# Cross-attention on one core: column maxima straight from PSUM in the first batch, and two block sums put behind the evictions

## Chip, cores and metric

The kernel runs on one core of a Trainium2 chip. The metric is the device time of one execution in microseconds (us). The engines are PE (matmuls), DVE (element-wise work on vectors), ACT (copies, exponentials, bias), POOL (reductions over partitions) and SP, which here only issues DMAs. Each engine runs its own queue in order.

## What is computed

The reference, cut to what matters; B = 8, C1 = C2 = 512, N = 1024, D = 64, all in fp32:

```python
q = einsum('bcn,dc->bnd', x1, Wq) + bq
k = einsum('bcn,dc->bdn', x2, Wk) + bk[:, None]
v = einsum('bcn,dc->bdn', x2, Wv) + bv[:, None]
attn = softmax(einsum('bnd,bdm->bnm', q, k), axis=2)
return einsum('bcm,bnm->bcn', v, attn) + x1
```

The kernel keeps the scores transposed: m lies on the partitions, in eight tiles of 128, and n on the columns, in two halves of 512. The softmax over m therefore needs a maximum and a sum over tiles and over partitions. It also multiplies in another order: y = x2 times the exponentials, scaled by the reciprocals of the sums, and then o = Wv y + bv + x1.

## The kernel before

Each batch is a `Batch` object `s` with its tiles. `head` (L349) does the first work of batch 0; then `period` (L431) runs once per batch and works on batch `s`, while it prepares the next one, `n`. The schedule is manual: the order in which the program issues instructions is the order of each engine's queue, and waits between engines follow from the tiles.

*Scores.* `scores(s, h, i)` (L164) makes the two score tiles of a pair: half h of the columns, pair i of 0 to 3, and groups g = 0, 1 of the rows, which come from the two row halves of PE at once (64 rows each). The pair goes either into one tile of the pool `ps_s`, which has two slots of two PSUM banks each (tag "sc"), or into two banks of the pool `ps_a`, "a0" and "a1" or "c0" and "c1". It returns `copy`, with which ACT moves the pair to SBUF, into `e[h]`; a pair in one tile takes one copy of 1024 columns (L189), a pair in two banks takes two of 512 (L187). All eight PSUM banks are used this way.

*Maximum and exponential.* `fold` (L194) takes the maximum (or the sum) of pairs 0 and i, two groups side by side, 1024 columns at once, on DVE (L201). `fold_halves` (L203) brings the two groups together (L205). `highest` (L207) does so and lets POOL reduce the result over the partitions (L210). Then the maximum is subtracted on DVE and ACT takes the exponential: `first_exponentials` for half 0 of batch 0 (L221, 512 columns each, L224 and L225), `exponentials` elsewhere (L227).

*Products.* The products y and o are made by a scheme of seven block products in place of eight (`MULT`, L259). Left blocks are quarters of x2 (`a`) or of Wv (`w`), with sums S1 to S4 (`left_sums`, L91; on DVE, L100); S3 is written over block 21, and S4 reads S2. Right blocks are quarters of the exponentials (`t`) or of y, with sums T1 to T4 (L233). `multiply` (L269) runs one block product into bank pair a or c of `ps_a`; `first(i)` and `second(i)` in `period` are the products for y and for o. The first product of y, `first(1)`, opens bank pair a, `first(2)` opens c. `evict_o(s, "12")` (L319) reads bank pair a and `evict_o(s, "21")` reads c, each with two instructions at L324; half 21 has two more additions at L331. Each eviction then issues its two stores on SP.

*The head.* `head` loads x1 of batch 0 into `x1_head` and x2 into `x2_head`, which holds the buffer of tag "e1". `head_queries` (L339) makes q of one half of the columns: eight matmuls, each in two passes on PE, in two column groups at once, then one ACT instruction that adds the bias (L347). Its bank is "c1" for half 0 and "a0" for half 1. The order in `head` from L384 is: q of half 0, the keys, the four pairs of scores of half 0 (pairs 0 and 1 in `ps_s`, pair 2 in a, pair 3 in c), the copy of pair 0, the first maximum with pair 1 read from PSUM, the copies of pairs 2, 3 and 1, two more maxima, `highest`, the sums S1 and S2, q of half 1, the load of x for the next batch, three pairs of scores of half 1, the eight exponentials of half 0, and last the copies of half 1. `first(1)` of `period` follows on PE and reads the first four exponentials.

*The end of a period.* In the first period the four sums S1 to S4 of the next batch stand at L529, after `evict_o(s, "22")` and ahead of the last two evictions. In later periods these sums are made earlier (L491 and L503).

Of the kernel before, what the change touches and what calls it, by code (L numbers as in the profile page):

```python
# [9 lines left out]
F32 = mybir.dt.float32  # L10
AF = mybir.ActivationFunctionType
ALU = mybir.AluOpType
# [3 lines left out]
def kernel(  # L16
# [40 lines left out]
    nc = tc.nc  # L57
    P = 128
    B, C, N = x1.shape
# [64 lines left out]
    def sum_a(s, *ks):  # L124
        for k in ks:
            if k != "S3":
                s.a[k] = sb.tile([P, MH, C // 2], F32, tag=f"a{k}", name=f"a{k}_{s.b}")
        left_sums(s.a, *ks)
# [35 lines left out]
    def scores(s, h, i, bank=None):  # L164


        if i == 0:
            s.e[h] = sb.tile([P, 2, MH, H], F32, tag=f"e{h}", name=f"e_{s.b}_{h}")
        e = s.e[h]
        if bank:  # L170
            whole = None
            ps = [
                ps_a.tile([P, H], F32, tag=f"{bank}{g}", name=f"ps_s{bank}{g}_{s.b}_{h}_{i}")
                for g in range(2)
            ]
        else:
            whole = ps_s.tile([P, 2, H], F32, tag="sc", name=f"ps_s_{s.b}_{h}_{i}")
            ps = [whole[:, g, :] for g in range(2)]
        for g, r in ((0, lo), (1, hi)):
            nc.tensor.matmul(  # L180
                ps[g], s.k[r, ts(i, P)], s.q[r, ts(h, H)], start=True, stop=True
            )

        def copy():
            if bank:
                for g in range(2):
                    nc.scalar.copy(e[:, g, i, :], ps[g])  # L187
            else:
                nc.scalar.copy(e[:, :, i, :], whole)  # L189

        copy.ps = whole
        return copy

    def fold(s, h, i, kind, op, ps=None):  # L194

        e = s.e[h]
        if i == 1:
            s.mx[h] = sb.tile([P, 2, H], F32, tag="fold", name=f"{kind}_{s.b}_{h}", bufs=2)
        f = s.mx[h]
        new = e[:, :, i, :] if ps is None else ps  # L200
        nc.vector.tensor_tensor(f, e[:, :, 0, :] if i == 1 else f, new, op)  # L201

    def fold_halves(s, h, op):  # L203
        f = s.mx[h]
        nc.vector.tensor_tensor(f[:, 0, :], f[:, 0, :], f[:, 1, :], op)  # L205

    def highest(s, h):  # L207
        fold_halves(s, h, ALU.max)
        s.top[h] = sb.tile([P, H], F32, tag="top", name=f"top_{s.b}_{h}", bufs=2)
        nc.gpsimd.partition_all_reduce(s.top[h], s.mx[h][:, 0, :], P, ReduceOp.max)  # L210

# [124 lines left out]
            fold(s, h, i, "sum", ALU.add)  # L336
        total(s, h)

    def head_queries(s, x_sb, h, bank):  # L339

        ps = ps_a.tile([P, H], F32, tag=bank, name=f"ps_q_{s.b}_{h}")
        for c in range(CT):
            for r in (lo, hi):
                nc.tensor.matmul(
                    ps[r, :], wq_sb[:, c, :], x_sb[:, c, ts(h, H)], start=(c == 0), stop=(c == CT - 1)
                )
        nc.scalar.activation(s.q[:, ts(h, H)], ps, AF.Identity, bias=bq_sb)  # L347

    def head(s):  # L349

        s.q = sb.tile([P, N], F32, tag="q", name=f"q_{s.b}", bufs=2)
        x1_sb = sb.tile([P, CT, N], F32, tag="x", name="x1_head")
        x2_sb = sb.tile([P, 2, MH, H], F32, tag="e1", name="x2_head")
        s.x = x2_sb.rearrange("p a (b t) n -> p (a b) (t n)", t=2)

        def load_x1(c, h):  # L360
            nc.sync.dma_start(
                x1_sb[:, c : c + 2, ts(h, H)],
                x1[s.b, c * P : (c + 2) * P, ts(h, H)].rearrange("(t p) n -> p t n", p=P),
            )

        nc.gpsimd.dma_start(bqk_sb, bqk)
        nc.gpsimd.dma_start(bv_sb, bv)
        nc.scalar.dma_start(wqk_sb, wqk)
        warm = const.tile([P, P], F32, name="warm")
        nc.vector.memset(warm, 0.0)  # L370
        ps = ps_a.tile([P, H], F32, tag="a0", name="ps_warm")
        for _ in range(WARM):
            nc.tensor.matmul(ps[:, 0:P], warm, warm, start=True, stop=True)
        load_x1(0, 0)
        load_x1(2, 0)
        for c in range(CT):
            nc.sync.dma_start(s.x[:, c, :], x2[s.b, ts(c, P), :])
        nc.scalar.activation(warm[:, 0:1], warm[:, 0:1], AF.Exp)
        load_a(s, "11")
        load_x1(0, 1)  # L380
        load_x1(2, 1)
        load_a(s, "21", "22", "12")
        load_values()
        head_queries(s, x1_sb, 0, "c1")  # L384
        keys(s, "c0")
        copies = [scores(s, 0, i, bank) for i, bank in enumerate((None, None, "a", "c"))]
        copies[0]()
        fold(s, 0, 1, "max", ALU.max, copies[1].ps)
        for i in (2, 3, 1):
            copies[i]()  # L390
        fold(s, 0, 2, "max", ALU.max)
        fold(s, 0, 3, "max", ALU.max)
        highest(s, 0)
        sum_a(s, "S1", "S2")
        head_queries(s, x1_sb, 1, "a0")
        load_x(states[1], x1)
        copies = [scores(s, 1, 0), scores(s, 1, 1), scores(s, 1, 2, "c")]
        for g in range(2):
            for i in range(MH):
                first_exponentials(s, g, i)  # L400
        for copy in copies:
            copy()
        fold(s, 0, 1, "sum", ALU.add)
        fold(s, 0, 2, "sum", ALU.add)
        fold(s, 1, 1, "max", ALU.max)
        fold(s, 0, 3, "sum", ALU.add)
# [24 lines left out]
    def period(s, n, nn, nnn):  # L431

        def first(i):
            multiply(s, "y", i, s.a, s.t, MH)

        def second(i):
            multiply(s, "o", i, w, s.y, 2)

        open_t(s)
        first(1)
        if s.b == 0:
            head_second(s, n)
        sum_e(s, "T1", "T2")
        if s.b == 0:
            total(s, 0)
        else:
            sum_e(s, "T4")
        if n:  # L450
            load_a(n, "11")
        first(2)
        if s.b == 0:
            keys(n)
            load_x(nn, x1)
            evict_y(s, "11", (1,))
            sum_e(s, "T4")
            shares(s, 0)
            evict_y(s, "11", (2,))
        else:  # L460
            shares(s, 0)
            evict_y(s, "11")
        sums(s, 1)
        sum_e(s, "T3")
        shares(s, 1)
        if n:
            load_a(n, "12", "21", "22")
        first(6)

        def next_queries():  # L470
            queries(nn)
            load_x(nn, x2)

        def next_keys():
            keys(nn)
            if nnn:
                load_x(nnn, x1)

        if n:
            scores_and(n, 0, "c", next_queries if nn else nothing)  # L480
            for i in range(1, MH):
                fold(n, 0, i, "max", ALU.max)
            highest(n, 0)
        first(5)
        fetch_o(s, "11")
        fetch_o(s, "22")
        if n:
            for i in range(MH):
                exponentials(n, 0, i)
            if s.b:  # L490
                sum_a(n, "S1", "S2", "S3")  # L491
        first(7)
        evict_y(s, "22")
        first(3)
        evict_y(s, "12")
        if n:
            scores_and(n, 1, "a", next_keys if nn else nothing)
            sums(n, 0)
        sum_y(s, "T1")
        sum_y(s, "T2")  # L500
        if n:
            if s.b:
                sum_a(n, "S4")  # L503
            else:
                left_sums(w, "S1", "S2", "S3", "S4")
            for i in range(1, MH):
                fold(n, 1, i, "max", ALU.max)
            highest(n, 1)
        first(4)
        evict_y(s, "21")  # L510
        second(1)
        sum_y(s, "T3")
        sum_y(s, "T4")
        second(6)
        fetch_o(s, "12")
        if n:
            exponentials(n, 1, 0)
            exponentials(n, 1, 1)
        second(2)
        evict_o(s, "11")  # L520
        fetch_o(s, "21")
        second(5)
        if n:
            exponentials(n, 1, 2)
            exponentials(n, 1, 3)
        second(7)
        evict_o(s, "22")
        if s.b == 0:
            sum_a(n, "S1", "S2", "S3", "S4")  # L529
        if n:  # L530
            second(3)
            evict_o(s, "12")
            second(4)
            evict_o(s, "21")
        else:
            second(4)
            evict_o(s, "21")
            second(3)
            evict_o(s, "12")
# [37 lines left out]
```

## Time and profile before

| | us |
|---|---|
| median of three runs | 717.13 (717.10 to 717.17) |
| the profiled execution | 716.93 |
| its span | 714.90 |
| granted clock of PE | 1.00 |
| DMA | 87.39 MB, mean 122 GB/s |

The span is the time from the first to the last instruction of the profiled execution; 2.03 us lie around it. A line of the timeline has start and duration in us, engine, line of the program, operation, written and read tiles, shape, number of instructions, and in brackets the idle time of the engine ahead of it with what ended it. What happens in the head, by the timelines of the engines: the last key matmul starts its group at 12.49, when its load has landed; the keys' bias on ACT ends at 14.31 and the scores of half 0 start at 14.36; q of half 1 runs from 17.99 and its bias from 21.70; POOL's reduction of the maximum takes 2.68 us from 21.72; the first exponential starts at 25.43 and the first product of y at 26.12.

### The profile page before, as it was taken

What the parts mean: (1) busy time and instruction counts of PE and PEld (TensorE: products, weight loads), DVE (VectorE), ACT (ScalarE), POOL (GpSimd) and SP (SyncE); (2) the same over time, 40 slices, a digit from 0 to 9 for tenths busy, and PEclk for the clock granted to TensorE, in tenths of its full rate; (3) what the DMA queues carried; (4) which work ended last, traced back from release to release, by engine and by line L of the source; (5) the groups of instructions that cost most, each with busy time, mean ns of one, the idle gap of its engine ahead of it and who ended that gap; (6) DMA issues with size and microseconds to landing.
All of it is one profiled execution on the core that took longest, in us unless ns stands there. A gap on an engine that the chain in (4) does not pass through costs nothing.

```text
span 714.9 us, 5407 instructions
## 1 busy us (share of the span) xinstructions
PE 705.6 (99%) x1892; PEld 299.8 (42%) x1892; DVE 590.2 (83%) x569; ACT 201.3 (28%) x271; POOL 97.2 (14%) x38
## 2 busy tenths in 40 slices
PE   8999999999999999999999999999999999999997
PEld 4333444434444434444344444443434444444443
DVE  0999899988979888798887987889887898989454
ACT  2733412043211522224231232403324034220010
POOL 0132030030200211021200202002020020301000
PEclk9999999999999999999999999999999999999999
DMA  8577132441333503435133252232601350042004
GB/s 333 210 235 256 68 147 101 156 154 46 147 146 119 189 8 141 148 118 191 58 119 127 109 191 98 108 118 89 220 0 61 117 177 0 0 161 75 0 1 147
DMA packets 34699, 87.39 MB, mean 122 GB/s; under 512 B 3952, under 2 KB 3952, under 8 KB 34672
## 3 DMA queue, kind: packets, MB, share of 16 engines
q1 hardware_dynamic: 33344, 84.95, 33.6%
q10 hardware_dynamic: 1264, 2.10, 0.9%
q8 instruction: 15, 0.25, 0.1%
q14 instruction: 12, 0.10, 0.0%
q0 software_dynamic: 64, 0.00, 0.0%
HBM read 68.42 MB, written 16.78 MB: 119 GB/s over the span
## 4 chain that ended last, share of the span: by engine, by line
PE 87%; DVE 8%; DMA 1%; issue 1%; ACT 1%; SPq 0%; POOL 0%; DVEq 0%; ACTq 0%; POOLq 0%
PE ps_ya L279 27%; PE ps_yc L279 21%; PE ps_oa L279 15%; PE ps_oc L279 11%; PE ps_s L180 5%; PE ps_k L138 3%; PE ps_q L138 3%; DVE max L201 1%; DMA x_head<-in_x_dram 1%; DVE eT L236 1%; DVE e L230 1%; DVE aS L100 1%; PE ps_sa L180 1%; DVE den L219 1%; PE ps_sc L180 1%
## 5 line engine op out<-in xcount | busy, mean ns | idle before, releaser
L215 POOL PARTITION_ALL_REDUCE den<-sum x16 | 65.3, 4081 | 433.2 <-DVE sum L205 433.2
L279 PE MATMUL ps_ya<-eT,aS 128*128 128x512 f32 x256 | 113.1, 595 | 0.0
L279 PE MATMUL ps_yc<-e,a 128*128 128x512 f32 x256 | 112.6, 592 | 0.0
L289 ACT COPY uy<-ps_ya 128x512 f32<-128x512 f32 x48 | 28.1, 588 | 233.2 <-PE ps_ya L279 233.2
L230 DVE TENSOR_TENSOR e<-e,top 128x1024 f32<-128x1024 f32 x60 | 70.0, 1219 | 13.9 <-POOL top L210 13.9
L279 PEld LDWEIGHTS ps_ya<-eT,aS 128*128 128x128 f32 x256 | 48.0, 190 | 63.8 <-issue 63.6
L279 PEld LDWEIGHTS ps_yc<-e,a 128*128 128x128 f32 x256 | 48.6, 190 | 61.6 <-issue 60.1
L324 DVE SCALAR_TENSOR_TENSOR o<-ps_oc,bv_sb,o 128x512 f32<-128x512 f32 x48 | 35.7, 749 | 41.6 <-PE ps_oc L279 41.5
L231 ACT ACTIVATE e<-e 128x1024 f32<-128x1024 f32 x60 | 62.2, 1056 | 22.2 <-DVE e L230 20.4
L289 ACT COPY uo<-ps_oa 128x512 f32<-128x512 f32 x48 | 28.1, 586 | 132.4 <-PE ps_oa L279 131.1
L189 ACT COPY e<-ps_s 128x1024 f32<-128x1024 f32 x47 | 46.7, 1027 | 61.5 <-PE ps_s L180 61.5
L279 PE MATMUL ps_ya<-e,a 128*128 128x512 f32 x128 | 56.4, 594 | 1.3 <-ACT e L225 0.8
L279 PE MATMUL ps_oc<-y,w 128*128 128x512 f32 x128 | 57.5, 592 | 0.0
L279 PE MATMUL ps_oa<-yT,w_S 128*128 128x512 f32 x128 | 57.5, 592 | 0.0
L279 PE MATMUL ps_yc<-eT,a 128*128 128x512 f32 x128 | 57.0, 598 | 0.0
L279 PE MATMUL ps_ya<-e,aS 128*128 128x512 f32 x128 | 56.2, 592 | 0.0
L219 DVE RECIPROCAL den<-den 128x512 f32<-128x512 f32 x16 | 53.6, 3349 | 0.0
L180 PE MATMUL ps_s<-q,k 64*128 64x512 f32 x188 | 47.9, 608 | 1.6 <-ACT q L347 0.8
L210 POOL PARTITION_ALL_REDUCE top<-max x16 | 30.3, 1897 | 131.3 <-DVE max L205 131.3
L308 DVE TENSOR_TENSOR y<-ps_yc,uy 128x512 f32<-128x512 f32 x48 | 31.2, 676 | 15.0 <-PE ps_yc L279 14.9
L201 DVE TENSOR_TENSOR max<-max,e 128x1024 f32<-128x1024 f32 x32 | 39.2, 1225 | 3.7 <-ACT e L187 0.5
L201 DVE TENSOR_TENSOR sum<-sum,e 128x1024 f32<-128x1024 f32 x32 | 39.2, 1225 | 2.1
(65 smaller groups left out, 757.5 us busy)
## 6 DMA issues: line engine op xcount, KB each, us to landing
x_in_x_dram<-in_x_dram SPq DMA_DIRECT2D x56, 512.0 KB, 5.4
a<-in_x2T_dram SPq DMA_DIRECT2D x32, 512.0 KB, 4.2
o<-in_x_dram SPq DMA_DIRECT2D x64, 256.0 KB, 6.4
out_dram<-o SPq DMA_DIRECT2D x64, 256.0 KB, 2.1
x_head<-in_x_dram SPq DMA_DIRECT2D x8, 512.0 KB, 8.0
q<-q ACTq DMA_DIRECT2D x14, 128.0 KB, 6.9
w<-in_wvT_dram SPq DMA_DIRECT2D x4, 256.0 KB, 8.9
wqk_sb<-in_wqk_dram ACTq DMA_DIRECT2D x1, 256.0 KB, 4.7
```

The source lines that it names most:

```text
L138: nc.tensor.matmul(ps[r, :], w_sb[:, c, :], s.x[:, c, ts(h, H)], start=(c == 0), stop=(c == CT - 1),)
L180: nc.tensor.matmul(ps[g], s.k[r, ts(i, P)], s.q[r, ts(h, H)], start=True, stop=True)
L189: nc.scalar.copy(e[:, :, i, :], whole)
L201: nc.vector.tensor_tensor(f, e[:, :, 0, :] if i == 1 else f, new, op)
L215: nc.gpsimd.partition_all_reduce(s.den[h], s.mx[h][:, 0, :], P, ReduceOp.add)
L219: nc.vector.reciprocal(s.rden[h], s.den[h])
L230: nc.vector.tensor_tensor(e, e, top, ALU.subtract)
L231: nc.scalar.activation(e, e, AF.Exp)
L279: nc.tensor.matmul(ps, left[ka][:, k, ts(j, P)], right[kb][:, k, :], start=opens and k == 0, stop=i in (2, 3, 4) and k == n_k - 1, skip_gr ...
L289: nc.scalar.copy(s.tmp[i, j], ps)
L308: nc.vector.tensor_tensor(y[:, j, :], ps, s.tmp[add, j], ALU.add)
L324: nc.vector.scalar_tensor_tensor(o, s.bank[bank, j], bv_sb[:, c : c + 1], o, ALU.add, ALU.add)
```

## The change

In the first batch, the maximum of half 0 is no longer taken pair by pair over 1024 columns. A new `head_max` takes it bank by bank over 512 columns: the first group of pair 0 is copied to SBUF and then the other seven banks are read from PSUM one after the other, always into the same tile. `fold_halves` is left out for this half, since both groups are then in one tile of 512 columns. The second group of pair 0 is copied by ACT after that, then pair 1; pairs 2 and 3 are handed over to the next step.

That step is the new `head_second_scores`. q of half 1 is made in two quarters of 256 columns, each in its own slot of `ps_s` instead of bank "a0". After the bias of each quarter stands the copy of one of the pairs 2 and 3 in ACT's queue. The scores of pairs 0 and 1 of half 1 are then made for the first 256 columns, and after that for the second 256; pair 2 is made as before. The sums S1 and S2 stand after these in the program instead of ahead of them, on DVE with nothing new between.

In the first period, S3 and S4 of the next batch move behind the last two evictions; S1 and S2 stay. This next batch is the second of the eight.

```diff
-        copy.ps = whole
+        copy.ps = ps
         return copy
 
-    def fold(s, h, i, kind, op, ps=None):
+    def fold(s, h, i, kind, op):
...
-        new = e[:, :, i, :] if ps is None else ps
-        nc.vector.tensor_tensor(f, e[:, :, 0, :] if i == 1 else f, new, op)
+        nc.vector.tensor_tensor(f, e[:, :, 0, :] if i == 1 else f, e[:, :, i, :], op)
...
+    def head_max(s, ps):
+
+        s.mx[0] = sb.tile([P, 2, H], F32, tag="fold", name=f"max_{s.b}_0", bufs=2)
+        f = s.mx[0][:, 0, :]
+        for i, new in enumerate(ps[1:]):
+            nc.vector.tensor_tensor(f, f if i else s.e[0][:, 0, 0, :], new, ALU.max)
+
     def highest(s, h):
-        fold_halves(s, h, ALU.max)
+        if s.b or h:
+            fold_halves(s, h, ALU.max)
...
-    def head_queries(s, x_sb, h, bank):
-
-        ps = ps_a.tile([P, H], F32, tag=bank, name=f"ps_q_{s.b}_{h}")
+    def head_queries(s, x_sb, n, ps):
+
         for c in range(CT):
             for r in (lo, hi):
                 nc.tensor.matmul(
-                    ps[r, :], wq_sb[:, c, :], x_sb[:, c, ts(h, H)], start=(c == 0), stop=(c == CT - 1)
+                    ps[r, :], wq_sb[:, c, :], x_sb[:, c, n], start=(c == 0), stop=(c == CT - 1)
                 )
-        nc.scalar.activation(s.q[:, ts(h, H)], ps, AF.Identity, bias=bq_sb)
+        nc.scalar.activation(s.q[:, n], ps, AF.Identity, bias=bq_sb)
+
+    def head_second_scores(s, x_sb, others):
+
+
+
+        halves = slice(H, H + H // 2), slice(H + H // 2, N)
+        for k, n in enumerate(halves):
+            ps = ps_s.tile([P, 2, H], F32, tag="sc", name=f"ps_q_{s.b}_{n.start}")
+            head_queries(s, x_sb, n, ps[:, 0, 0 : H // 2])
+            others[k]()
+        s.e[1] = sb.tile([P, 2, MH, H], F32, tag="e1", name=f"e_{s.b}_1")
+        ps = [ps_s.tile([P, 2, H], F32, tag="sc", name=f"ps_s_{s.b}_1_{i}") for i in range(2)]
+        for k, n in enumerate(halves):
+            for i in range(2):
+                for g, r in ((0, lo), (1, hi)):
+                    nc.tensor.matmul(
+                        ps[i][:, g, ts(k, H // 2)],
+                        s.k[r, ts(i, P)],
+                        s.q[r, n],
+                        start=True,
+                        stop=True,
+                    )
+        last = scores(s, 1, 2, "c")
+
+        def copy():
+            for i in range(2):
+                nc.scalar.copy(s.e[1][:, :, i, :], ps[i])
+            last()
+
+        return copy
...
-        head_queries(s, x1_sb, 0, "c1")
+        head_queries(s, x1_sb, slice(0, H), ps_a.tile([P, H], F32, tag="c1", name="ps_q_head"))
         keys(s, "c0")
         copies = [scores(s, 0, i, bank) for i, bank in enumerate((None, None, "a", "c"))]
-        copies[0]()
-        fold(s, 0, 1, "max", ALU.max, copies[1].ps)
-        for i in (2, 3, 1):
-            copies[i]()
-        fold(s, 0, 2, "max", ALU.max)
-        fold(s, 0, 3, "max", ALU.max)
+        e, ps = s.e[0], copies[0].ps
+        nc.scalar.copy(e[:, 0, 0, :], ps[0])
+        head_max(s, sum((c.ps for c in copies), []))
+        nc.scalar.copy(e[:, 1, 0, :], ps[1])
+        copies[1]()
+        copy = head_second_scores(s, x1_sb, copies[2:])
         highest(s, 0)
         sum_a(s, "S1", "S2")
-        head_queries(s, x1_sb, 1, "a0")
         load_x(states[1], x1)
-        copies = [scores(s, 1, 0), scores(s, 1, 1), scores(s, 1, 2, "c")]
         for g in range(2):
             for i in range(MH):
                 first_exponentials(s, g, i)
-        for copy in copies:
-            copy()
+        copy()
...
         if s.b == 0:
-            sum_a(n, "S1", "S2", "S3", "S4")
+            sum_a(n, "S1", "S2")
         if n:
             second(3)
             evict_o(s, "12")
             second(4)
             evict_o(s, "21")
+            if s.b == 0:
+                sum_a(n, "S3", "S4")
```

## The prediction

> **What bounds the kernel now.** I read the busy times first, then the list of waits of PE, then the chain of waits in the first batch, and last the timeline of DVE and PE at the end of the first period.
>
> ```profile
> span 714.9 us, 5407 instructions
> ...
> PE 705.6 (99%) x1892; PEld 299.8 (42%) x1892; DVE 590.2 (83%) x569; ACT 201.3 (28%) x271; POOL 97.2 (14%) x38
> ```
>
> PE is busy for 99% of the span, so a gain can only be a gap of PE that closes. The list of waits (total, times, longest, in us) names the gaps:
>
> ```profile
> PE ps_ya L279 <- ACT e L225: 0.8, 1, 0.8
> PE ps_s L180 <- ACT q L347: 0.8, 1, 0.8
> ...
> PE ps_ya L279 <- DVE o L324: 0.5, 1, 0.5
> ...
> PE ps_sa L180 <- DVE y L306: 0.2, 1, 0.2
> ```
>
> After 130 us PE waits for nothing. So whatever PE gains before 130 us reaches the end, unless DVE work made late there becomes a new wait. The first two waits lie in the first batch. The chain of waits there (start, us, what):
>
> ```profile
> 18.34 1.24 DVE max L201
> ...
> 19.67 1.24 DVE max L201
> ...
> 21.54 1.23 DVE aS L100
> ...
> 22.79 1.94 DVE aS L100
> 24.74 0.61 DVE e L224
> ...
> 25.43 1.77 ACT e L225 x3
> ```
>
> The reader is to see two things. From the maxima the path runs over DVE (S1, S2, the first subtraction) and ACT's first exponential to PE's first y product at 26.12. And two maxima of which the second reads what the first wrote start 1.33 us apart, though each takes 1.226: the wait of DVE for its own result, next to a wait for another engine (here ACT), costs 0.105. The third wait sits at the end of the first period; DVE and PE in the timeline:
>
> ```profile
> 120.65 1.22 DVE L100 TENSOR_TENSOR a<-a,a 128x1024 f32<-128x1024 f32 x1
> 121.78 1.22 DVE L100 TENSOR_TENSOR aS<-a,aS 128x1024 f32<-128x1024 f32 x1
> 122.92 1.40 DVE L324 SCALAR_TENSOR_TENSOR o<-ps_oa,bv_sb,o 128x512 f32<-128x512 f32 x2
> ```
> ```profile
> 119.61 3.60 PE L279 MATMUL ps_oc<-yT,w 128*128 128x512 f32 x8
> 123.72 7.13 PE L279 MATMUL ps_ya<-e,a 128*128 128x512 f32 x16 [0.51 <-DVE o L324]
> ```
>
> The two lines of L100 are S3 and S4 of the next batch (S1 and S2 ran from 118.25): they stand ahead of the evictions that free PE's bank.
>
> [...]
>
> **Part A, maxima of half 0.** Removed on DVE: three maxima of 1024 columns (16.58 to 20.90, with a hole of 0.54 for an ACT copy) and the fold of halves at 20.93 (0.69). Added: seven maxima of 512 columns, each reading the result of the one before. The first needs half of the first copy: 15.54 + 0.586 (L187, the same shape) + 0.03 = 16.16, against 16.58. The banks are ready before their turn: PE finishes the last score at about 18.1. So the chain's pace decides. A maximum takes 0.68 to 0.69 and waits for DVE's own result and for a PE result that no earlier wait covers: 0.685 + 0.105 = 0.79. The seventh starts at 16.16 + 6 x 0.79 = 20.90 and ends at 21.58; the old fold ended at 21.62. S1 follows 0.60 after the seventh's start, at 21.50 (before 21.54), and POOL's reduction after its end. Gain about 0.05.
>
> The pace is no row of this trace, so bounds: if only DVE's own wait is paid, it is 0.71 (the w sums, 95.25 to 95.96), and S1 starts at 21.02, a gain of 0.5. If nothing is waited for it is 0.60 (L306, two independent ones), and the gain is 1.17. Below, 0.80 with a duration of 0.692 loses 0.02. I take 0.79, because each reading instruction is an in-place update like L201's, where the price was paid.
>
> The order behind it is unchanged: S1, S2 (stretched to 1.94 beside POOL's 2.68), subtraction 3.12 after S1's start, exponential 0.77 later, PE 0.68 after that. All move by the same 0.05.
>
> **Part A, q of half 1 and the scores in halves of columns.** It must only be done before PE is wanted at 26.07. Passes of 512 columns come every 0.43, the last of 128 columns in the warm-up 0.13 apart; 256 columns I put at 0.215, half of 0.43. PE starts q at 17.99 as before (its slot is free at 17.5: the first maximum ends 16.84, ACT's second copy follows). The first half's eight pairs end at about 19.8, the second's last pass starts at 21.32. On ACT, in queue order: the whole copy of pair 1 waits for maximum 3 (18.4) and ends 19.5; bias of q's first half 20.0 to 20.5 (0.689 less 256 columns, 0.21); two copies of pair 2 to 21.5; second half 21.75 to 22.2; two copies of pair 3 to 23.2. Behind them stand the exponentials, due at 25.4: cover 2.2. On PE scores (1,0) start at 21.63, (1,1) after q's second half at 22.27, and (1,2), whose banks ACT frees at 23.2, has its last pass at 24.09. PE is ready at 24.6, 1.45 before the exponential. So the wait for q (0.8) goes, but what is late next is the exponential: worth nothing. No DMA is added; the next batch's x load waits on the same reads of x1_head, whose end stays at 21.7. Inputs are no limit: S1 ran without a DMA wait at 21.54.
>
> **Part B, S3 and S4 of the next batch last.** The two sums at 120.65 and 121.78 (2.27) go behind both evictions. Eviction 12 then starts at 120.65, its banks having been complete since 119.8, and both are free at 122.06, before PE's last pass of second(4) (starting 122.62). The y product starts at 123.05 instead of 123.72, without the first weight load exposed (passes 0.53 apart at that start, 0.43 otherwise): gain 0.67 + 0.10 = 0.77.
>
> What comes late: eviction 21 waits for second(4) to 123.26; two additions of o to 125.2; S3 125.1, S4 126.25, and T1 at 127.4 instead of 126.75, while PE is 0.77 early. T2 is due at first(6), 136.8, and is done at about 132.9: cover 3.9. The rest of DVE runs 0.65 late until it waits for PE anyway, 0.48 at 169.20 and 2.74 at 172.64; there 1.42 is absorbed. S3 is needed at 158, S4 at 165. SP's queue gets its two output stores for half 12 earlier. Without that cover the price would be at most 1.42.
>
> **Sum.** 0.05 + 0.77 = 0.82. The profiled execution took 716.93 (span 714.90 and 2.03 around it), becoming 716.1; the median, 0.20 higher, 717.13 - 0.82 = 716.3.
>
> **Rivals.** No change within what can be told is 0.2%, 1.43 us, so 715.70 to 718.56.
>
> 1. The forecast, 716.3: 0.48.
> 2. The maxima run at 0.71, one wait each: 717.13 - 0.5 - 0.77 = 715.85. For it: the PE results are long there, so that wait may overlap. Against: at L201 the queue paid for both. 0.19.
> 3. They run at 0.60: 717.13 - 1.17 - 0.77 = 715.2; PE would still be ready (24.6) before the exponential (24.9). Against: in-place sums in the trace never come closer than 0.71 at 512. 0.18.
> 4. The period's gain is given back, because DVE, late by 1.42 relative to PE, makes PE wait further on: 717.1. For it: DVE was the late one at 85.95 and 123.72. Against: the cover counted above. 0.07.
> 5. Slower: narrow passes cost more than half. There are 24 pair passes of 256 columns (16 of q, 8 of scores). Extra of 0.06 each uses up PE's 1.45; from 0.095 each the whole change loses; if a pass costs as much as one of 512 columns, 24 x 0.215 - 1.45 = 3.7 is lost, 717.13 + 3.7 - 0.77 = 720.1. For it: weights must load within 0.215, and loads take 0.137 to 0.187. Against: passes 0.13 apart in the warm-up with loads of 128 columns. 0.08.
>
> **Numbers.** Faster by over 0.2%: rival 3 and what of 1 and 2 lies under 715.70, 0.35. Slower: 0.08. Same: 0.57. For eight in ten, from rival 3's edge to rival 4's: 715.0 to 717.0. The forecast's own range is 716.0 to 716.5.
>
> **What would show it.** The seven maxima in the timeline of DVE: 0.79 apart, the last starting near 20.9. The first y product near 26.07, with its wait for the exponential grown from 0.8 to about 1.4, and no wait of scores for q longer than 0.3. At the end of the first period no wait for an eviction. The T sums start 4.4 us after the y product instead of 3.0, and no new PE wait up to 175. Wrong: maxima closer than 0.75, q passes further than 0.25 apart, or a new PE wait after 124.

## The result and the profile after

The changed kernel took 716.26 us (median of 20 runs) against 717.15 for the kernel before (20 runs): a ratio of 0.9986, 95% interval 0.9980 to 0.9992. That is 0.89 us faster, where the forecast was 716.3 and a gain of 0.82. The gain is 0.12%, under the 0.2% that the prediction took as its bound for no change, though with so many runs the interval leaves out 1. The rest of this document is about where the 0.89 lies, and whether it lies where the steps of the prediction put it.

The page of the changed kernel (its span, then busy time, share and instructions of each engine):

```profile
span 714.4 us, 5460 instructions
...
PE 705.5 (99%) x1916; PEld 301.4 (42%) x1916; DVE 590.6 (83%) x572; ACT 201.8 (28%) x273; POOL 97.2 (14%) x38
```

PE's busy time is as before (705.5 and 705.6), with 24 matmuls more: the passes of 256 columns. The span is only 0.5 shorter. But the first scores start at 14.68 here and at 14.36 in the profile before, because the loads of the head landed later in this execution (the last key matmuls, which wait for one, start at 12.81 instead of 12.49). That start varied from 14.36 to 14.83 over the profiles of this study, whatever the kernel, and no part of the change can reach it: all of its work comes after. So I compare places by their distance from the start of the first score matmul (L180), not by the clock of the span.

The list of waits of PE (total, times, longest, in us):

```profile
PE ps_ya L286 <- ACT e L232: 1.3, 1, 1.3
...
PE ps_s L180 <- ACT k L162: 0.8, 1, 0.8
...
PE ps_k L138 <- DMA x_head<-in_x_dram: 0.2, 1, 0.2
```

Of the four waits shown of before, the one for q (0.8) and the one for the eviction (0.5) are gone, and the one for the first exponential grew from 0.8 to 1.3. The one for y (ps_sa, 0.2) is no longer listed, though it is not gone: y12_early, below, takes it up. The wait for the exponential is the first batch's only large wait that the change could touch, and it took over what the wait for q gave up. The chain of waits in the first batch (start, us, what) shows what stands behind it:

```profile
16.47 0.70 DVE max L211
...
17.20 0.02 DVEq L211
...
17.27 0.70 DVE max L211
...
17.99 0.70 DVE max L211
...
18.72 0.02 DVEq L211
...
18.78 0.70 DVE max L211
```

The reader is to see the price of a wait. From one maximum to the next it is 0.80, 0.72 and 0.79. Between the first two and the last two stands a piece "DVEq" of 0.02: in five of the six steps the queue of DVE has an instruction of its own, 21 ns long, for a second wait. By the semaphores in the trace, that piece waits for DVE's own result and the maximum behind it waits for PE. Between the second and the third there is none (that maximum waits for DVE's own result alone), and the step is about 0.07 shorter. The seventh maximum starts at 21.16, which is 6.48 after the first scores; the prediction had 6.54.

At the end of the first period, DVE and PE in the timeline (start, length, engine, line, operation, tiles, count, and in brackets the idle time ahead and its releaser):

```profile
120.87 1.40 DVE L331 SCALAR_TENSOR_TENSOR o<-ps_oa,bv_sb,o 128x512 f32<-128x512 f32 x2
122.19 0.74 DVE L331 SCALAR_TENSOR_TENSOR o<-ps_oc,bv_sb,o 128x512 f32<-128x512 f32 x1
123.47 0.75 DVE L331 SCALAR_TENSOR_TENSOR o<-ps_oc,bv_sb,o 128x512 f32<-128x512 f32 x1 [0.54 <-PE ps_oc L286]
...
125.34 1.22 DVE L100 TENSOR_TENSOR a<-a,a 128x1024 f32<-128x1024 f32 x1
126.48 1.22 DVE L100 TENSOR_TENSOR aS<-a,aS 128x1024 f32<-128x1024 f32 x1
127.61 1.22 DVE L243 TENSOR_TENSOR eT<-e,e 128x1024 f32<-128x1024 f32 x1
```

```profile
119.84 3.60 PE L286 MATMUL ps_oc<-yT,w 128*128 128x512 f32 x8
123.27 7.03 PE L286 MATMUL ps_ya<-e,a 128*128 128x512 f32 x16
```

The evictions of ps_oa now start 2.4 us before PE's y product, and that product starts with no idle time ahead of it. Its group is 7.03 long where it was 7.13: the first weight load starts at 122.84, 0.43 ahead of the first pass, and the second pass comes 0.43 after the first; before, load and pass started together (123.71 and 123.72) and the second pass came 0.53 after the first. S3 and S4 end at 127.70, and the T sums start 4.34 us after the y product (3.03 before; 4.4 was predicted). DVE is late there, and has made up for it some 45 us further on:

```profile
169.29 0.68 DVE L313 TENSOR_TENSOR y<-ps_ya,den 128x512 f32<-128x512 f32 x1
172.09 0.69 DVE L313 TENSOR_TENSOR y<-ps_ya,den 128x512 f32<-128x512 f32 x1 [2.12 <-PE ps_ya L286]
```

Where DVE waited 0.48 and 2.74 us for PE before, it waits 0 and 2.12: the lateness went into idle time of DVE, and PE waits for nothing after 124 us.

### The profile page after: what moved, and what is told of

It is laid out like the page before. It is cut to its first block, busy times and chain, and to the rows that moved or that the text cites. A ratio compares the mean times of both kernels' runs of the same rounds, so it can differ in the third digit from the quotient of the medians.

```text
span 714.4 us, 5460 instructions
## 1 busy us (share of the span) xinstructions
PE 705.5 (99%) x1916; PEld 301.4 (42%) x1916; DVE 590.6 (83%) x572; ACT 201.8 (28%) x273; POOL 97.2 (14%) x38
## 4 chain that ended last, share of the span: by engine, by line
PE 88%; DVE 8%; DMA 1%; ACT 1%; issue 1%; SPq 0%; POOL 0%; DVEq 0%; ACTq 0%; POOLq 0%
PE ps_ya L286 27%; PE ps_yc L286 21%; PE ps_oa L286 15%; PE ps_oc L286 12%; PE ps_s L180 5%; PE ps_k L138 3%; PE ps_q L138 3%; DMA x_head<-in_x_dram 1%; DVE eT L243 1%; DVE e L237 1%; DVE max L200 1%; PE ps_sa L180 1%; DVE den L226 1%; DVE aS L100 1%; PE ps_sc L180 1%
## 5 line engine op out<-in xcount | busy, mean ns | idle before, releaser
L189 ACT COPY e<-ps_s 128x1024 f32<-128x1024 f32 x44 | 43.7, 1027 | 60.0 <-PE ps_s L180 59.1
L180 PE MATMUL ps_s<-q,k 64*128 64x512 f32 x180 | 45.9, 607 | 0.8 <-ACT k L162 0.8
L243 DVE TENSOR_TENSOR eT<-e,eT 128x1024 f32<-128x1024 f32 x32 | 38.9, 1255 | 0.5
```

Source lines behind the costliest of these rows:

```text
L180: nc.tensor.matmul(ps[g], s.k[r, ts(i, P)], s.q[r, ts(h, H)], start=True, stop=True)
L243: nc.vector.tensor_tensor(t[k], t[x], t[y], ALU.subtract)
```

## The experiments

All times are medians, each beside that of the kernel before, timed together with it. The ratio is taken over the runs themselves and can differ a little from the quotient of the medians. Distances are from the first score matmul in the profiled execution: to the first y product, to the keys that PE makes in the middle of the first period (the group of L138 near 88 us), to the first y product of the second period, and to the start of the last matmul.

| kernel | us | before | ratio, 95% interval | first y | keys | second y | last matmul |
|---|---|---|---|---|---|---|---|
| before | | 717.15 | | 11.76 | 74.10 | 109.36 | 695.55 |
| after | 716.26 | 717.15 | 0.9986 [0.9980, 0.9992] | 11.60 | 74.00 | 108.59 | 694.68 |
| a_only | 717.05 | 717.12 | 1.0004 [0.9996, 1.0012] | 11.60 | 73.99 | 109.24 | 695.43 |
| b_only | 716.46 | 717.12 | 0.9992 [0.9984, 1.0001] | 11.75 | 74.07 | 108.66 | 694.75 |
| unsplit | 716.24 | 717.12 | 0.9987 [0.9980, 0.9993] | 11.59 | 73.97 | 108.56 | 694.65 |
| two_chains | 715.65 | 717.12 | 0.9982 [0.9975, 0.9988] | 10.95 | 73.33 | 107.92 | 694.01 |
| y12_early | 715.42 | 717.20 | 0.9974 [0.9964, 0.9983] | 11.60 | 72.92 | 107.51 | 693.60 |
| both | 714.70 | 717.20 | 0.9965 [0.9952, 0.9977] | 10.94 | 72.21 | 106.80 | 692.89 |
| all_last | 716.39 | 717.20 | 0.9991 [0.9982, 0.9999] | 11.59 | 73.98 | 108.57 | 694.66 |
| both_unsplit | 714.79 | 717.23 | 0.9967 [0.9954, 0.9979] | 10.95 | 72.41 | 107.00 | 693.09 |
| s2_late | 715.01 | 717.23 | 0.9972 [0.9961, 0.9982] | 10.73 | 72.79 | 107.38 | 693.47 |

### One part at a time: a_only and b_only

a_only is the changed kernel with the order of S1 to S4 put back:

```diff
-            sum_a(n, "S1", "S2")
+            sum_a(n, "S1", "S2", "S3", "S4")
...
-            if s.b == 0:
-                sum_a(n, "S3", "S4")
```

> The changed kernel with part B undone: the new head, S3 and S4 ahead of the evictions again. My theory: 0.05 to 0.2 us faster than before, 716.95 to 717.1, with the wait for the eviction (0.5) back. Rival, that the head gives the gain: about 716.3.

b_only is the kernel before with the same two places changed the other way.

> The kernel before with part B alone: S3 and S4 of the next batch go behind the last two evictions, the head stays as it was. My theory, that most of the gain is the wait for eviction 12 at the end of the first period: 0.7 to 0.8 us faster than before, about 716.4, no PE wait for an eviction at 123, the wait of scores for q (0.8) still there. Rival, that the gain is the head's closed wait for q: no faster than 717.0.

The ratios alone don't settle how the gain is divided: both intervals reach 1, and a gain of 0.1 can't be told from none in the medians. The distances and the waits do. The list of waits of a_only:

```profile
PE ps_ya L286 <- ACT e L232: 1.3, 1, 1.3
...
PE ps_ya L286 <- DVE o L331: 0.5, 1, 0.5
```

and of b_only:

```profile
PE ps_ya L279 <- ACT e L225: 0.8, 1, 0.8
...
PE ps_s L180 <- ACT q L347: 0.8, 1, 0.8
...
PE ps_sa L180 <- DVE y L306: 0.3, 1, 0.3
```

With part A alone the wait for the eviction stands as before, and the last matmul comes 0.12 earlier. With part B alone the head's waits stand, and the last matmul comes 0.80 earlier. Together 0.92; the changed kernel has 0.87. So the parts add, and B is nine tenths of the change.

### Are the narrow pieces worth anything: unsplit

The changed kernel with q of half 1 and its scores made over 512 columns again, in one slot of ps_s, between the copies of pairs 2 and 3:

```diff
-        for k, n in enumerate(halves):
-            ps = ps_s.tile([P, 2, H], F32, tag="sc", name=f"ps_q_{s.b}_{n.start}")
-            head_queries(s, x_sb, n, ps[:, 0, 0 : H // 2])
-            others[k]()
...
+        others[0]()
+        ps = ps_s.tile([P, 2, H], F32, tag="sc", name=f"ps_q_{s.b}_1")
+        head_queries(s, x_sb, slice(H, N), ps[:, 0, :])
+        others[1]()
+        copies = [scores(s, 1, 0), scores(s, 1, 1), scores(s, 1, 2, "c")]
```

> The changed kernel with q of half 1 and its scores in whole columns (512) again; q takes a slot of the score pool, its bias stands between ACT's copies of pairs 2 and 3. My theory, that PE has 1.4 us to spare ahead of the first exponential: the same time as the changed kernel (within 0.1 us), the wait for q back at about 0.8 and the wait for the exponential down from 1.3 to about 0.7. Rival, that the narrow pieces carry the head's gain: 0.8 us slower than the changed kernel, the wait for the exponential as it was.

It takes 716.24, the same as the change within what can be told, and its first y product is at 11.59 instead of 11.60. Its waits of PE:

```profile
PE ps_s L180 <- ACT q L353: 0.8, 1, 0.8
PE ps_ya L286 <- ACT e L232: 0.7, 1, 0.7
```

The wait for q is back with its 0.8, and the wait for the exponential is shorter by 0.6. The sum of the two (1.5) is near the 1.3 of the change: two waits in a row before one deadline trade against each other, and DVE's and ACT's path to the exponential sets where they end.

### What a cheaper chain of maxima gives: two_chains

The maxima as two chains, one for each group of a pair, so that every second instruction is independent of the one before; the fold of the halves comes back, and ACT copies both groups of pair 0 first:

```diff
-        f = s.mx[0][:, 0, :]
-        for i, new in enumerate(ps[1:]):
-            nc.vector.tensor_tensor(f, f if i else s.e[0][:, 0, 0, :], new, ALU.max)
+        f = s.mx[0]
+        for i in range(1, MH):
+            for g in range(2):
+                old = s.e[0][:, g, 0, :] if i == 1 else f[:, g, :]
+                nc.vector.tensor_tensor(f[:, g, :], old, ps[2 * i + g], ALU.max)
```

> The changed kernel with the maxima of half 0 in two chains, one for each group, taken in turn, and the fold of halves after them: again seven instructions of 512 columns, but only the last reads the result of the one just before it; ACT copies both groups of pair 0 first. My theory, that DVE's wait for its own result sets the pace: maxima 0.61 apart, first y product about 0.9 us earlier, 715.4. Rival, that reading PSUM or the waits for PE set the pace of 0.79: maxima still 0.7 to 0.8 apart, no gain, 716.3 or, with the copy of the second group ahead, later.

```profile
16.68 1.28 DVE L213 TENSOR_TENSOR max<-e,ps_s 128x512 f32<-128x512 f32 x2 [15.68 <-PE ps_s L180]
17.88 1.28 DVE L213 TENSOR_TENSOR max<-max,ps_sa 128x512 f32<-128x512 f32 x2
19.07 1.27 DVE L213 TENSOR_TENSOR max<-max,ps_sc 128x512 f32<-128x512 f32 x2
20.38 0.69 DVE L204 TENSOR_TENSOR max<-max 128x512 f32<-128x512 f32 x1
```

This is DVE's timeline of two_chains. Pairs of maxima start 1.20 apart, 0.60 for each instead of 0.79. The first starts 2.12 after the first scores instead of 1.79, since it now waits for PE's second pair; that is why the gain at the first product is 0.65 and not the 0.9 that I had expected. All of the 0.65 reaches the last matmul (694.01 against 694.68), and the median is 0.61 below the change's. This answers the question that the prediction left between its forecast and its rival of 0.60 a step: the path over DVE's maxima does set the first product, and the change as written pays 0.79 on it for five of its six steps.

### The wait that the list makes small: y12_early

What part A and two_chains gain at the first product meets another wait further on: near 86 us PE waits for DVE. The list puts it at 0.2 to 0.4, and in the profile after it isn't in the list at all. PE's timeline there, of before and then of after:

```profile
83.76 1.99 PE L180 MATMUL ps_s<-q,k 64*128 64x512 f32 x8
...
88.46 3.65 PE L138 MATMUL ps_k<-x_in_x_dram,wqk_sb 128*64 128x512 f32 x16
```

```profile
84.08 1.99 PE L180 MATMUL ps_s<-q,k 64*128 64x512 f32 x8
86.18 1.29 PE L180 MATMUL ps_sa<-q,k 64*128 64x512 f32 x3
87.14 0.59 PE L180 MATMUL ps_s<-q,k 64*128 64x512 f32 x1
...
87.57 1.19 PE L180 MATMUL ps_s<-q,k 64*128 64x512 f32 x3
88.68 3.65 PE L138 MATMUL ps_k<-x_in_x_dram,wqk_sb 128*64 128x512 f32 x16
```

Sixteen passes take 4.70 before (83.76 to 88.46) and 4.60 after (84.08 to 88.68), with the records drawn out and out of turn. The same passes in the next period of the kernel before take 3.63 (172.53 to 176.16). DVE scales the "22" part of y (L317) ahead of its eviction of "12" (L313), which frees the bank ps_sa. In y12_early the eviction goes first, in the first period only:

```diff
-        evict_y(s, "22")
+        evict_y(s, "22", (1, 2) if s.b else (1,))
         first(3)
         evict_y(s, "12")
+        if s.b == 0:
+            evict_y(s, "22", (2,))
```

> The changed kernel; in the first period alone the scaling of y block 22 by the reciprocals goes behind the eviction of y block 12, which frees PE's bank pair a. By the trace PE loses about 1 us at 86 to that eviction, though the list of waits shows 0.2 or nothing. My theory: the scores group at 84 takes 3.6 us as in later periods in place of 4.6, and all of it reaches the end: 715.2 to 715.4. Rival, that DVE's lateness only comes out later, at y block 21 for second(2) or at the last evictions of the period: 716.0 or more, with a new PE wait between 100 and 125.

PE's timeline of y12_early:

```profile
83.87 1.99 PE L180 MATMUL ps_s<-q,k 64*128 64x512 f32 x8
85.69 1.02 PE L180 MATMUL ps_sa<-q,k 64*128 64x512 f32 x4
...
87.50 3.65 PE L138 MATMUL ps_k<-x_in_x_dram,wqk_sb 128*64 128x512 f32 x16
```

The same sixteen passes take 3.63, so 0.97 had been lost where the list named at most 0.4. To the last matmul it is 1.08 less than the change (the keys of the second batch, near 45 us, which take 3.63 to 4.11 from one execution to another, with the landing of their x load as the likely reason, since s2_late lists a wait of 0.21 for it there, blur such a difference by a tenth or more); the median, 715.42, is 0.84 less.

This also explains what part A keeps. At the first product A is 0.16 ahead of before, at the keys near 88 only 0.10. In between, PE's own lead counts for nothing: at the scores near 84, just ahead of the wait, a_only is 0.23 ahead of before (69.17 after the first scores instead of 69.40) and the change is level with it (69.41, since the keys of the second batch took 3.95 in that execution instead of 3.79), yet behind the wait both are 0.1 ahead. What both share is DVE's lead: its first subtraction, which heads DVE's queue into this wait, is 0.10 earlier (10.20 after the first scores instead of 10.30), and its eviction of "12" is 0.09 and 0.11 earlier (70.76 and 70.74 instead of 70.85). So in these runs it is DVE's lead, and not PE's, that reaches the end.

### The two together: both

> Two chains of maxima and the early eviction of y block 12 together. If both gains lie on PE's path one after the other, they add: 716.3 - 0.9 - 1.0 = 714.4. Rival, that DVE is the limit of the first period whatever is done at its ends: not more than the better of the two alone, about 715.3.

both has the edits of two_chains and of y12_early. It has the lowest time of the kernels that ran: 714.70, a ratio of 0.9965 [0.9952, 0.9977] to the kernel before. The 714.4 that I had expected rested on 0.9 for the two chains, which gave 0.65. Its last matmul is 1.79 earlier than the change's, against 0.67 and 1.08 for the two alone: they add, and no new wait took their place.

### How much lateness DVE can bear: all_last

The changed kernel with all four sums of the second batch behind the evictions:

```diff
-        if s.b == 0:
-            sum_a(n, "S1", "S2")
...
-                sum_a(n, "S3", "S4")
+                sum_a(n, "S1", "S2", "S3", "S4")
```

> The changed kernel with all four sums S1 to S4 of the next batch behind the last two evictions. It tests the cover that the prediction counted for sums that come late: S2 and T2 are due for first(6) of the second period, and DVE comes 2.3 us later to them than in the changed kernel. My theory, cover of 3.9 us: the same time as the changed kernel within 0.2 us, no new PE wait. Rival, that the sums come back as a wait: a PE wait for DVE near 137 or 165, 717.0 or more.

DVE's timeline of all_last:

```profile
128.86 1.22 DVE L100 TENSOR_TENSOR aS<-a,aS 128x1024 f32<-128x1024 f32 x1
130.00 1.22 DVE L243 TENSOR_TENSOR eT<-e,e 128x1024 f32<-128x1024 f32 x1
```

The T sums start at 130.00, 2.4 later than in the change, and nothing is lost: the last matmul is at 694.66 (694.68), the median 0.13 above the change's, inside both intervals. So the cover after the second y product is at least 2.4 us more than part B uses. The place of S3 and S4 is not finely balanced.

### Narrow pieces when the head is shorter: both_unsplit

both with the queries and scores of unsplit. The question was whether the narrow pieces pay once the exponential comes 0.65 earlier.

> Two chains and the early eviction together, with q of half 1 and its scores in whole columns of 512 again. In the run with whole columns before, PE was ready 0.7 us ahead of the exponential; two chains brought that forward by 0.66. My theory: PE is just in time, the same as with narrow pieces, 714.6 to 714.9, the wait for the exponential gone. Rival, that narrow pieces pay once the exponential is early: 715.2 or more, with the wait for q in place of that for the exponential.

714.79 against 714.70, the first y product at 10.95 against 10.94. PE waits 0.8 for q and no longer for the exponential. PE just keeps up, and the narrow pieces are worth at most 0.1 even here. The 0.20 that this profile has more than both at the keys near 88 and after came in with the keys of the second batch near 45 us (3.97 instead of 3.78), whose length varies as said above.

### A miss: s2_late

both, and S2 of the first batch moved behind the eight first subtractions, with all of the "22" part of y behind "12" in the first period:

```diff
-        sum_a(s, "S1", "S2")
+        sum_a(s, "S1")
...
                 first_exponentials(s, g, i)
+        sum_a(s, "S2")
         copy()
```

> Two chains and the early eviction together; S2 of batch 0 moves behind the eight first subtractions, so that only S1 lies beside POOL's reduction, and in the first period the whole eviction of y block 22 goes behind that of block 12. If POOL's reduction and S2 are what the exponential waits for: the first product 0.6 us earlier, where PE is ready, 714.0 to 714.3. Rival, that DVE, whose work is only moved, is then late somewhere in the first period and gives it back: 714.6 or more, with a new PE wait for DVE between 80 and 110.

It took 715.01, 0.31 more than both (the intervals of the two ratios overlap): my expectation failed. The rival's time held, but not its place, for it had put a new wait for DVE between 80 and 110 us. The timeline of s2_late, DVE and POOL:

```profile
20.92 1.22 DVE L100 TENSOR_TENSOR aS<-a,a 128x1024 f32<-128x1024 f32 x1
21.10 2.68 POOL L218 PARTITION_ALL_REDUCE top<-max  x1 [18.45 <-DVE max L204]
...
23.82 2.50 DVE L232 TENSOR_TENSOR e<-e,top 128x512 f32<-128x512 f32 x4 [1.68 <-POOL top L218]
```

I had put the length of POOL's reduction down to S2 beside it. With S2 gone it still takes 2.68, and DVE stands idle for 1.68; S1 still runs beside it; no run took that away. The first product comes only 0.21 earlier than in both, and this is given back: PE waits 0.2 for the x load of its keys at 47 and 0.2 for a T sum at 50, two waits that both doesn't have. That T sum ends 0.8 later than in both, on a DVE queue that now holds S2 ahead of it. At the scores near 84 s2_late is 0.57 behind both (69.15 after the first scores instead of 68.58), and at the last matmul 0.58: the moved "22", which comes behind those scores, costs nothing that the profile shows. Of the loss, 0.33 came in with the keys near 45 us (4.11 instead of 3.78), whose length varies from one execution to another, and 0.47 with the y product behind them, which holds the wait for the T sum (7.53 instead of 7.06); 0.21 had been gained.

## Why the prediction was right, step by step

**Part A, the maxima.** Right in mechanism: a step of the chain pays for DVE's own result and for a PE result, 0.79. One of the six steps has no second wait and takes 0.72, under the 0.75 that the prediction had named as a sign of being wrong, so the seventh starts 6.48 after the first scores and not 6.54. The rivals of 0.71 and 0.60 a step are out for this kernel; 0.60 was measured with independent neighbours, in two_chains.

**Part A, the path behind them.** The prediction moved everything by the same 0.05. S1 came 0.10 earlier (7.08 after the first scores instead of 7.18), the subtraction too, and the first product 0.16: the exponential starts 0.71 after the subtraction instead of 0.77. In the chain before, a piece "ACTq" stands ahead of that exponential:

```profile
25.37 0.02 ACTq L225
```

In the chain after there is none:

```profile
24.96 0.61 DVE e L231
25.57 0.02 issue
25.59 1.83 ACT e L232 x3
```

So one wait of two has gone. By the semaphores in the traces it is the one for ACT's own earlier work; the one for DVE stays. Of 0.16, 0.12 is at the end in a_only. The term was mis-sized by 0.07. Its route was not the predicted one either: the prediction held that whatever PE gains before 130 us reaches the end, but ahead of the wait near 86 only what DVE gained does, as the section on y12_early shows. For part A the two happened to be of like size.

**The copies on ACT.** The prediction has ACT's copy of pair 1 wait for DVE's third maximum, which reads the same bank. That was an assumption: in the profile before, the copy of pair 1 starts at 19.15, long after the maximum of its banks (16.58 to 17.80), and shows no such wait. ACT's timeline of after bears it out:

```profile
17.19 0.59 ACT L426 COPY e<-ps_s 128x512 f32<-128x512 f32 x1 [0.75 <-DVE max L211]
18.71 1.01 ACT L189 COPY e<-ps_s 128x1024 f32<-128x1024 f32 x1 [0.93 <-DVE max L211]
```

Both instructions only read these banks, and each copy starts 0.03 after the maximum that it waits for has ended (those of 16.47 and 17.99, each 0.69 long). The wait is one that the program carries, a semaphore of DVE's ahead of each copy. The copies ended at 23.47 and the exponentials begin at 25.59: the predicted cover of 2.2 was 2.1.

**The narrow passes.** PE's timeline of after:

```profile
18.31 3.67 PE L350 MATMUL ps_q<-x_head,wqk_sb 128*64 128x256 f32 x32
21.91 2.21 PE L369 MATMUL ps_s<-q,k 64*128 64x256 f32 x16
...
26.28 7.13 PE L286 MATMUL ps_ya<-e,a 128*128 128x512 f32 x16 [1.29 <-ACT e L232]
```

From the start of q to the start of the scores is 3.60 for 16 pairs of passes, 0.225 each: the first step is 0.27, the 14 behind it are 0.216, and from the last pass to the scores, where the tiles turn from 128*64 to 64*128, it is 0.31; 0.215 was taken. Half of the 0.43 of 512 columns was the right estimate; the 0.13 of the warm-up, which the prediction set beside it, is one step, the last, and the 17 ahead of it are 0.213. The eight pairs of score passes take 2.05 (21.91 to 23.96), for three of them start 0.32 after the one before, not 0.216. In all that is about 0.5 more than 24 times 0.215, inside the cover of 1.45. The rival on the other side needed 0.095 more for each of the 24, some 2.3. As predicted, the wait for q goes and is worth nothing, for the exponential is late next (1.29; some 1.4 had been put).

**Part B.** 0.67 for the start of the product and 0.10 for its first weight load, 0.77 in all. The stretch from the keys near 88 to the second y product is 35.26 before and 34.59 after, which is the 0.67, and 7.13 became 7.03, which is the 0.10. b_only has 0.80 at the end. The rival that DVE's lateness gives it back is out: T sums 4.34 after the product, 0 and 2.12 idle left at 169 and 172, and in all_last a further 2.4 to spare. Of DVE's idle time there 1.10 was used up, where the prediction had 1.42.

**The sum.** 0.05 and 0.77 were put; 0.12 and 0.77 to 0.80 were measured, by the last matmul. The carrying term, part B, was right in mechanism and in size. That the median came within 0.04 of the forecast, closer than part A was sized, is in part luck.

## What to carry to other kernels

When a wait on the bounding engine goes, look at what its next deadline is before counting the gain: here the wait for q was worth nothing in front of a later wait for an exponential, while 2.27 us of sums that needn't be there yet, moved behind two evictions, gave nearly all. Count the instructions of a dependent chain by their start to start, not by their length (0.79 here for a length of 0.69), and break the chain in two where it sets the path (0.60 then). A lead of the bounding engine ahead of such a later wait for another engine counts only as far as that engine is earlier too: of a_only's 0.23 ahead of the wait near 86, 0.1 was left behind it. And measure a suspected wait by the length of its stretch against the same stretch in a later period: the list of waits named 0.4 where nearly 1 us was to be had.

## What the runs showed of the hardware that was not expected

A maximum of 128x512 that takes 0.68 to 0.69 starts 0.60 after the one before it in two_chains, where it doesn't read that one's result. In after it starts 0.72 after the one before it where it reads that one's result (0.71 for a sum of this shape, 95.48 to 96.19), and 0.79 to 0.80 where it also has a second wait. In two_chains the maxima from the third on also read a result of DVE's and a bank that PE wrote, but the result is one instruction older, and the step is still 0.60.

POOL's reduction of a maximum takes 2.68 and 2.69 the first two times and 1.78 the other fourteen. The kernel before:

```profile
21.72 2.68 POOL L210 PARTITION_ALL_REDUCE top<-max  x1 [19.06 <-DVE max L205]
37.71 2.69 POOL L210 PARTITION_ALL_REDUCE top<-max  x1 [13.30 <-DVE max L205]
...
76.44 1.78 POOL L210 PARTITION_ALL_REDUCE top<-max  x1 [8.03 <-DVE max L205]
```

Beside each of the two long ones DVE runs block sums of 128x1024, the first of which had started 0.18 earlier; beside the other fourteen it runs none. With S2 taken away (s2_late) the first still takes 2.68, with S1 beside it, so S1 may be the cause; that wasn't tested. In the changed kernel S2 took 1.95 beside the reduction instead of 1.22: it started 1.08 after POOL and ended 0.35 after POOL's end (POOL: 2.68 from 21.94), by the profile's rough spans of POOL. The two scalings of y at L317 that run beside the reduction at 102.77 take 0.68 each, as elsewhere, with the reduction at 1.78. What makes the first two reductions longer stays open.
